# Layer 0 cross-attention: query scaling moved to ScalarE, the second normalisation rewritten as two VectorE operations per tile, beta added to x in advance

## The chip, the core and the metric

The kernel runs on one core of a Trainium2 chip. The metric is the device time of one execution in microseconds (us), given as the median of several executions. Engines are named as in the profile: PE is TensorE's matmul side and PEld its weight loads, DVE is VectorE, ACT is ScalarE, POOL is GpSimd, and SP is SyncE, which here issues DMAs only.

## The reference

The program is a decoder of four layers, each with self-attention, cross-attention and a feed-forward part, on x of 16 batches x 128 tokens x 256 channels in float32. Only the cross-attention of layer 0 is changed. Its part of the reference, where `query` is the layer-normalised x and `key` and `value` are both the context of 16 x 128 x 192:

```python
Qp = query @ Wq + bq
K = _l2norm(key @ Wk + bk)
V = value @ Wv + bv
Q = _l2norm(Qp)
# split into 16 heads of 16
scores = einsum('bhqd,bhkd->bhqk', Q, K) * SCALE        # SCALE = 1/4
attn = softmax(scores, axis=-1)
out = einsum('bhqk,bhkd->bhqd', attn, V)
out = out @ Wo + bo
x = out + Qp
mu = mean(x); var = mean((x - mu) ** 2)
return (x - mu) / sqrt(var + LN_EPS) * ln_gamma + ln_beta
```

The decoder adds the returned value to its own x: `x = x + _L0_xattn_ref(_layernorm(x), ...)`. The length of a query is taken over all 256 channels, before the split into heads.

## The kernel before

**Tiling.** The 16 batches are 16 tiles of 128 tokens (tokens on the partitions, 256 channels along the free side). Four tiles make a group; x lives in SBUF as four buffers `x[0]` to `x[3]`, one for each group, of 128 x 1024 float32 elements. In the built program they appear as x_70, x_72, x_74 and x_76.

**Stages.** `staggered` drives both attentions of layer 0. For each group a generator `prologue(g)` makes keys, values and queries, in pieces that are run between the steps of the group before it. For each tile, `scores16` gives the scores `st` on PE, `exponentials16` the exponentials `e` on ACT (L330, two instructions of 128 x 1024), and `combine16` in four pieces the weighted values `o`, their copy `oT` on ACT (L356), the transposition `o16t`, the division by the row sums on DVE (`rsum` L364, `c` L365), the transposition `ctr`, its copy `cT` on DVE (L373), the product `proj`, and `done(ps)`, which takes the product out of PSUM.

**The prologue of the cross-attention.** `stats` takes mean and variance of x for two groups at a time (L526, L527, buffers `l1mv` and `l1rs`); h is the normalised x (L546). After kT (L555, with the squares `ksq` on ACT, L556), the transposes `tr` of h and the sums of squares of the keys, the queries `qp` = hT x Wq + bq come out of PSUM on DVE (L579), and ACT sums their squares (L580). The reciprocal lengths `n` take a maximum (L583), a square root on ACT (L584) and a reciprocal (L585). `unit` is qp divided by its length, four DVE instructions (L588). POOL then adds bo to qp (L589). PE transposes unit (`utr`), and DVE and ACT write it to `qm`, masked for even and odd heads (L605, L606).

**The end of a group.** `done` adds the product to qp (L616). After the fourth tile, `norm_tokens` normalises qp (L203, L204 for statistics, L193 for the root on ACT, L194 for the reciprocal, L207 for four DVE instructions), and POOL multiplies with gamma (L619), adds beta (L620) and adds the result to x (L621), each in one instruction over the whole group.

**What follows.** `l0_ffn_rows(g)` normalises the new x for the feed-forward part: statistics on DVE (L643, L644), `nmean` (L646), h on ACT (L649), transposes `tr` on PE, and copies `hT` on ACT (L657). It is called for groups 0 and 1 within the cross-attention and for 2 and 3 at the start of the feed-forward part, which then runs gate, up and down products for 33 sets of weights.

**What sets the order.** The functions `pinned` and `pinned_transpose` keep PE in the order in which the program is written. For the other engines a scheduler orders the instructions by a model of when they are ready, and each engine then works through its own queue in order. Small buffers come from a pool (`small`) with four buffers for each name and shape; `bnst` and `bnmv` are such names, shared by `stats` (`bnst` alone), `norm_tokens` and `l0_ffn_rows`. PSUM has four one-bank buffers (`b1`), used in turn by kT, tr, qp, v, utr, o, o16t, ctr and proj, and two two-bank buffers (`b2`) for the scores.

Of the kernel before, what the change touches and what calls it, by code (L numbers as in the profile page):

```python
# [12 lines left out]
AF = mybir.ActivationFunctionType  # L13
ALU = mybir.AluOpType
# [3 lines left out]
P = 128  # L18
B = 16
T = B * P  # L20
DM = 256
DC = 192
NG = 4
GB = B // NG
# [6 lines left out]
class Decoder:  # L31
# [479 lines left out]
    def l0_xattn(self):  # L511
        nc = self.nc
        wq, wk_, wv, wo = self.load4(["L0_xattn_Wq", "L0_xattn_Wk", "L0_xattn_Wv", "L0_xattn_Wo"])
        gamma, beta = self.b("ln_gamma"), self.b("ln_beta")
        T4 = lambda t: slice(t * P, (t + 1) * P)

        rows, qps = {}, []

        def stats(gs):
            n = len(gs)  # L520
            bs = self.small([P, GB, 6], "bnst")
            mv = self.small([P, n, GB, 2], "l1mv")
            rs = self.small([P, n, GB], "l1rs")
            for i, g in enumerate(gs):
                for t in range(GB):
                    nc.vector.bn_stats(bs[:, t, :], self.x[g][:, t, :])  # L526
                    nc.vector.bn_aggr(mv[:, i, t, :], bs[:, t, :])  # L527
            self.rsqrt(rs, mv[:, :, :, 1])
            for i, g in enumerate(gs):
                rows[g] = mv[:, i], rs[:, i]  # L530

        def products(out, pairs):
            for i, (l, r) in enumerate(pairs):
                self.pinned(out, l, r, start=i == 0, stop=i == len(pairs) - 1)

        with self.tc.tile_pool(name="l0x", bufs=1) as wk:
            bq, bv, bo = (self.brow(wk, f"L0_xattn_{n}") for n in ("bq", "bv", "bo"))

            def prologue(g):

                if g in (0, 2):
                    stats([g, g + 1])
                mv, rs = rows[g]
                h = self.hp.tile([P, GB, DM], F, tag="h", name="h", bufs=2)
                for t in range(GB):
                    nc.vector.tensor_scalar(  # L546
                        h[:, t, :], self.x[g][:, t, :], mv[:, t, 0:1], rs[:, t : t + 1], ALU.subtract, ALU.mult
                    )

                kT = wk.tile([P, 2, GT], F, tag="kT", name="kT", bufs=2)  # L550
                sq = self.hp.tile([P, 2, GT], F, tag="hT", name="ksq", bufs=5)
                for half in range(2):
                    ps = self.b1("kT")
                    products(ps, self.ctx_l(wk_, half * P, (half + 1) * P, slice(g * GT, (g + 1) * GT)))
                    nc.vector.tensor_scalar(kT[:, half, :], ps, self.c("L0_xattn_bk")[:, half : half + 1], None, ALU.add)  # L555
                    nc.scalar.activation(sq[:, half, :], kT[:, half, :], AF.Square)  # L556
                    yield
                hT = self.hp.tile([P, 2, GT], F, tag="hT", name="hT", bufs=5)
                for k in range(2):
                    ps = self.b1("tr")  # L560
                    for t in range(GB):
                        self.pinned_transpose(ps[:, T4(t)], h[:, t, k * P : (k + 1) * P])
                    self.evac(hT[:, k, :], ps)

                n = self.small([P, 2, GB], "lengths")
                ps = self.b1("ksum")[:, 0:GB]
                for t in range(GB):
                    products(ps[:, t : t + 1], [(sq[:, half, T4(t)], self.ones[:, 0:1]) for half in range(2)])

                nc.vector.tensor_scalar(n[:, 0], ps, 1e-24, 16.0, ALU.max, ALU.mult)  # L570
                yield
                if g % 2 == 0:
                    qps.append(self.slot([P, 2, GB, DM], "qp"))
                qp = qps[-1][:, g % 2]
                junk = wk.tile([P, DM], BF, tag="junk", name="junk", bufs=1)
                for t in range(GB):
                    ps = self.b1("qp")[:, 0:DM]
                    products(ps, [(hT[:, k, T4(t)], wq[:, k, :]) for k in range(2)])
                    nc.vector.tensor_tensor(qp[:, t, :], ps, bq, ALU.add)  # L579
                    nc.scalar.activation(junk, qp[:, t, :], AF.Square, accum_out=n[:, 1, t : t + 1])  # L580
                    if t == 1:
                        yield
                nc.vector.tensor_scalar(n[:, 1], n[:, 1], 1e-24, None, ALU.max)  # L583
                nc.scalar.activation(n, n, AF.Sqrt)  # L584
                nc.vector.reciprocal(n, n)  # L585
                u = self.hp.tile([P, GB, DM], F, tag="h", name="unit", bufs=2)
                for t in range(GB):
                    nc.vector.tensor_scalar(u[:, t, :], qp[:, t, :], n[:, 1, t : t + 1], None, ALU.mult)  # L588
                nc.gpsimd.tensor_tensor(qp, qp, bo.unsqueeze(1).to_broadcast([P, GB, DM]), ALU.add)  # L589
                yield  # L590
                v = []

                def values(t):
                    pairs = self.ctx_r(wv, 0, DM, slice(g * GT + t * P, g * GT + (t + 1) * P))
                    v.append(self.values32(wk, pairs, bv, products))

                values(0)
                values(1)
                yield
                qm = wk.tile([P, 2, 2, GT], F, tag="qm", name="qm", bufs=2)  # L600
                for half in range(2):
                    ps = self.b1("utr")
                    for t in range(GB):
                        self.pinned_transpose(ps[:, T4(t)], u[:, t, half * P : (half + 1) * P])
                    nc.vector.tensor_scalar(qm[:, half, 0, :], ps, self.par[:, 0:1], None, ALU.mult)  # L605
                    nc.scalar.activation(qm[:, half, 1, :], ps, AF.Copy, scale=self.par[:, 1:2])  # L606
                yield
                values(2)
                values(3)
                return qm, kT, n[:, 0], v, qp  # L610

            def combine(s, g, t, es):
                qp = s[4]

                def done(ps):
                    nc.vector.tensor_tensor(qp[:, t, :], qp[:, t, :], ps, ALU.add)  # L616
                    if t == GB - 1:
                        self.norm_tokens(qp, qp)
                        nc.gpsimd.tensor_tensor(qp, qp, gamma.unsqueeze(1).to_broadcast([P, GB, DM]), ALU.mult)  # L619
                        nc.gpsimd.tensor_tensor(qp, qp, beta.unsqueeze(1).to_broadcast([P, GB, DM]), ALU.add)  # L620
                        nc.gpsimd.tensor_tensor(self.x[g], self.x[g], qp, ALU.add)  # L621

                return self.combine16(wk, es, s[3][t], wo, done)


            self.staggered(
                prologue,
                None,
                lambda s, t: self.scores16(s[0], s[1], T4(t), False),
                lambda s, t, st, nm: self.exponentials16(wk, st, s[2][:, t : t + 1], None),  # L630
                combine,
                {13: [lambda: self.l0_ffn_rows(0)], 14: [lambda: self.l0_ffn_rows(1)]},
            )
# [1944 lines left out]
```

## Time and profile before

| | |
|---|---|
| median of 3 runs | 3607.33 us (3598.66 to 3616.08) |
| profiled execution | 3604.5 us, its span 3602.7 us |
| granted PE clock over the span | 0.962 |
| PE, DVE, ACT, POOL busy | 92%, 59%, 39%, 12% of the span |
| cross-attention of layer 0 | about 181 to 368 us from the span's start |

A position such as "261.55" is in us from the start of the span. In the timeline a line holds start, duration, engine, source line, operation, output and inputs, and in brackets how long the engine sat idle before it and what released it. In the list of groups a line ends with busy us, mean ns of one, and the idle time before the group with what ended most of it. In the windows view each stretch lists the busy us of PE, PEld, DVE, ACT and POOL with the number of instructions, and then the granted PE clock, the DMA share and GB/s. In the list of waits, the numbers are total us, times, and the longest.

### The profile page before, as it was taken

How to read it: one execution, taken by the hardware profiler on the slowest of the kernel's cores; microseconds unless marked ns; L12 is line 12 of the kernel's file. 1: busy time of each engine (PE TensorE's matmuls, PEld its weight loads, DVE VectorE, ACT ScalarE, POOL GpSimd, SP SyncE). 2: the span in 40 equal slices, each digit the busy share in tenths (PEclk: the TensorE clock that was granted, in tenths of full speed). 3: DMA queues.
4: the chain of work that ended last, by engine and by line, in shares of the span. 5: the costliest groups of instructions: out<-in, count | busy, mean ns of one | idle time of the engine just before them, and what ended most of it. 6: DMA issues, size and time to landing. Idle time of an engine off the chain costs nothing.

```text
span 3602.7 us, 51438 instructions
## 1 busy us (share of the span) xinstructions
PE 3305.2 (92%) x20947; PEld 1789.6 (50%) x20947; DVE 2117.7 (59%) x4185; ACT 1415.6 (39%) x1904; POOL 443.5 (12%) x613
## 2 busy tenths in 40 slices
PE   7888999999998899998899999297999999999999
PEld 4655555555556556674455565162222222224656
DVE  5555444444463544558777644426999999963430
ACT  2345311111124422228555323023677767783221
POOL 5422000000003321110000110104000000002100
PEclk9988999999999999999999999597999999999989
DMA  2000000000110100000100000374212020000000
GB/s 77 1 23 10 18 18 18 22 18 18 32 49 2 38 1 1 1 31 20 46 1 13 2 1 1 137 229 126 38 26 32 11 32 12 11 1 26 1 8 18
DMA packets 90500, 105.46 MB, mean 29 GB/s; under 512 B 11380, under 2 KB 72694, under 8 KB 90006
## 3 DMA queue, kind: packets, MB, share of 16 engines
q1 hardware_dynamic: 79672, 89.71, 9.6%
q0 software_dynamic: 4224, 6.43, 0.6%
q10 hardware_dynamic: 6368, 6.03, 0.5%
q8 instruction: 165, 2.70, 0.3%
q14 instruction: 71, 0.58, 0.1%
HBM read 85.53 MB, written 16.60 MB: 28 GB/s over the span
## 4 chain that ended last, share of the span: by engine, by line
PE 78%; DVE 9%; ACT 5%; issue 4%; DMA 2%; POOL 1%; SPq 0%; POOLq 0%; ACTq 0%; DVEq 0%
PE acc L2110 7%; PE down L257 6%; PE gate L257 6%; PE up L257 6%; PE proj L257 6%; PE st L2110 5%; PE one L2110 4%; PE st L257 4%; PE qT L168 4%; PE o L257 3%; PE h L257 2%; DVE mx L2256 2%; PE rb L257 2%; PE fc L168 2%; PE pr L168 2%
## 5 line engine op out<-in xcount | busy, mean ns | idle before, releaser
L2256 DVE TENSOR_REDUCE mx<-one 128x1 f32<-128x512 f32 x1024 | 658.4, 686 | 56.6 <-PE one L2110 47.6
L2393 ACT ACTIVATE e<-st 128x1024 f32<-128x1024 f32 x512 | 497.1, 1021 | 206.5 <-PE st L2110 205.3
L748 ACT ACTIVATE gs<-gate,cols 128x512 f32<-128x512 f32 x132 | 90.7, 687 | 553.1 <-PE gate L257 553.1
L2110 PE MATMUL acc<-e,v 128*32 128x512 f32 x2048 | 283.7, 608 | 1.2 <-ACT e L2393 1.2
L762 DVE SCALAR_TENSOR_TENSOR x<-down,w_all,x 128x256 f32<-128x256 f32 x512 | 212.4, 477 | 110.5 <-PE down L257 110.4
L2110 PE MATMUL st<-qp,kp 113*128 113x512 bf16 x1024 | 270.5, 384 | 5.9 <-DMA qp<-shifts 3.4
L257 PE MATMUL down<-expert,gs 128*128 128x256 f32 x1056 | 250.1, 380 | 2.2 <-DVE gs L749 2.2
L257 PE MATMUL gate<-hT,expert 128*128 128x512 f32 x528 | 250.1, 596 | 0.0
L257 PE MATMUL up<-hT,expert 128*128 128x512 f32 x528 | 248.1, 592 | 0.0
L257 PEld LDWEIGHTS down<-expert,gs 128*128 128x128 f32 x1056 | 200.8, 190 | 85.8 <-issue 61.5
L749 DVE SCALAR_TENSOR_TENSOR gs<-up,cols,gs 128x512 f32<-128x512 f32 x132 | 99.0, 750 | 234.2 <-PE up L257 229.1
L2110 PE MATMUL one<-kp,qp 16*128 16x512 bf16 x1024 | 210.7, 395 | 3.7 <-DVE mx L2256 2.4
L2110 PEld LDWEIGHTS <-qp 16*128 16x128 bf16 x1024 | 48.8, 91 | 326.0 <-issue 321.1
L257 PEld LDWEIGHTS up<-hT,expert 128*128 128x128 f32 x528 | 100.3, 190 | 126.4 <-issue 126.4
L2110 PEld LDWEIGHTS <-kp 113*128 113x128 bf16 x1024 | 78.8, 98 | 142.3 <-issue 80.5
L1120 ACT COPY rb<-rb 128x512 f32<-128x512 f32 x64 | 37.5, 585 | 256.6 <-PE rb L257 256.6
L257 PEld LDWEIGHTS gate<-hT,expert 128*128 128x128 f32 x528 | 100.6, 192 | 70.9 <-issue 64.4
L1122 DVE TENSOR_TENSOR cT<-o,rb 128x512 f32<-128x512 f32 x64 | 44.2, 691 | 154.9 <-ACT rb L1120 154.9
L168 PE MATMUL qT<-hT,L_xattn_Wq 128*128 128x512 f32 x256 | 115.7, 605 | 6.8 <-DVE hT L112 4.5
L257 PE MATMUL o<-e,v 128*32 128x128 f32 (+1 forms) x2048 | 105.4, 279 | 13.7 <-DVE nm L294 11.8
L1429 DVE SCALAR_TENSOR_TENSOR xs<-xBC,cols,xs 128x508 f32<-128x508 f32 x144 | 106.0, 741 | 12.4 <-ACT xs L1425 9.0
L257 PEld LDWEIGHTS o<-e,v 128*32 128x32 f32 (+1 forms) x2048 | 81.5, 124 | 29.7 <-POOL e L335 12.3
(536 smaller groups left out, 5417.3 us busy)
## 6 DMA issues: line engine op xcount, KB each, us to landing
W<-in_L_ffn_W_dram SPq DMA_DIRECT2D x46, 512.0 KB, 5.6
expert<-in_L_ffn_Wg_dram SPq DMA_DIRECT2D x32, 128.0 KB, 2.2
expert<-in_L_ffn_Wu_dram SPq DMA_DIRECT2D x32, 128.0 KB, 2.4
expert<-in_L_ffn_Wd_dram SPq DMA_DIRECT2D x32, 128.0 KB, 2.5
parts<-parts SPq DMA_DIRECT2D x16, 256.0 KB, 3.9
qp<-parts SPq DMA_DIRECT2D x28, 128.0 KB, 3.8
kp<-parts SPq DMA_DIRECT2D x12, 256.0 KB, 8.7
hs<-zero SPq DMA_DIRECT2D x23, 128.0 KB, 1.8
```

The source lines that it names most:

```text
L168: self.nc.tensor.matmul(out, lhsT, rhs, start=i == 0, stop=i == n - 1 and bias is None)
L257: self.tc.keep_in_program_order(self.nc.tensor.matmul(*a, **k))
L748: nc.scalar.activation(gs, pg, AF.Silu, bias=bg)
L749: nc.vector.scalar_tensor_tensor(gs, pu, bu, gs, ALU.add, ALU.mult)
L762: nc.vector.scalar_tensor_tensor(xt, pd[:, t, :], w_all[:, o : o + 1], xt, ALU.mult, ALU.add)
L1120: nc.scalar.copy(rb, ps)
L1122: nc.vector.tensor_tensor(cT, po, rb, ALU.mult)
L1429: stt = lambda *a: pin(nc.vector.scalar_tensor_tensor(*a))
L2110: self.tc.keep_in_program_order(nc.tensor.matmul(*a, **k))
L2256: nc.vector.tensor_reduce(mx[:, t, kc, i : i + 1], pair[i], AX.X, ALU.max)
L2393: nc.scalar.activation(e[:, 2 * p : 2 * p + 2, :], ps, AF.Exp, scale=1.0 / 16.0)
```

## The change

The four instructions that write `unit` move from DVE to ACT. The three POOL instructions at a group's end go. In their place every tile, right after its product is added, takes its statistics and is rewritten as (qp - mean) x gamma on DVE; after the fourth tile the reciprocal deviation is computed, and four DVE instructions add qp x rstd to x. Beta is added to x on POOL in the prologue, after h has been taken from x. The buffers `bnst` and `bnmv` of a group are now taken at its first tile rather than after its fourth.

```diff
-        rows, qps = {}, []
+        rows, qps, norms = {}, [], {}
...
                 for t in range(GB):
-                    nc.vector.tensor_scalar(u[:, t, :], qp[:, t, :], n[:, 1, t : t + 1], None, ALU.mult)
+                    nc.scalar.activation(u[:, t, :], qp[:, t, :], AF.Copy, scale=n[:, 1, t : t + 1])
                 nc.gpsimd.tensor_tensor(qp, qp, bo.unsqueeze(1).to_broadcast([P, GB, DM]), ALU.add)
+                nc.gpsimd.tensor_tensor(self.x[g], self.x[g], beta.unsqueeze(1).to_broadcast([P, GB, DM]), ALU.add)
...
                 def done(ps):
                     nc.vector.tensor_tensor(qp[:, t, :], qp[:, t, :], ps, ALU.add)
+                    if t == 0:
+                        norms[g] = self.small([P, GB, 6], "bnst"), self.small([P, GB, 2], "bnmv")
+                    st, mv = norms[g]
+                    nc.vector.bn_stats(st[:, t, :], qp[:, t, :])
+                    nc.vector.bn_aggr(mv[:, t, :], st[:, t, :])
+                    nc.vector.scalar_tensor_tensor(
+                        qp[:, t, :], qp[:, t, :], mv[:, t, 0:1], gamma, ALU.subtract, ALU.mult
+                    )
                     if t == GB - 1:
-                        self.norm_tokens(qp, qp)
-                        nc.gpsimd.tensor_tensor(qp, qp, gamma.unsqueeze(1).to_broadcast([P, GB, DM]), ALU.mult)
-                        nc.gpsimd.tensor_tensor(qp, qp, beta.unsqueeze(1).to_broadcast([P, GB, DM]), ALU.add)
-                        nc.gpsimd.tensor_tensor(self.x[g], self.x[g], qp, ALU.add)
+                        rs = self.small([P, GB], "rstd")
+                        self.rsqrt(rs, mv[:, :, 1])
+                        for i in range(GB):
+                            xt = self.x[g][:, i, :]
+                            nc.vector.scalar_tensor_tensor(xt, qp[:, i, :], rs[:, i : i + 1], xt, ALU.mult, ALU.add)
```

In the changed file the lines shift a little: unit stays L588, bo on POOL stays L589, beta on POOL is L590, the masked copies are L606 and L607, the addition of the product is L617, the statistics L621 and L622, the multiplication with gamma L623, the addition to x L631. In `l0_ffn_rows` the statistics become L653 and L654, nmean L656 and h L659.

## The prediction

> **What bounds the kernel now.** I read the chain first, then PE's waits in the stage that changes, then the timeline around the longest of them, and last the windows for the granted clock. The chain of the whole execution is PE's:
>
> ```profile
> PE 78%; DVE 9%; ACT 5%; issue 4%; DMA 2%; POOL 1%; SPq 0%; POOLq 0%; ACTq 0%; DVEq 0%
> ```
>
> So only what makes PE wait counts. PE's list of waits from 197 to 370 us has eight rows, 31.2 us together; three carry it:
>
> ```profile
> PE tr L260 <- ACT h L649: 12.8, 2, 7.2
> PE proj L257 <- DVE cT L373: 7.0, 4, 5.4
> PE proj L257 <- DVE rstd L194: 5.4, 1, 5.4
> ```
>
> None of the engines named is short of time; the timeline of the second row shows what is behind it:
>
> ```profile
> 259.96 2.36 POOL L619 TENSOR_TENSOR qp<-qp,bcast 128x1024 f32<-128x1024 f32 x1 [0.66 <-DVE lengths L583]
> 261.55 6.02 DVE L588 TENSOR_SCALAR unit<-qp,lengths 128x256 f32<-128x256 f32 x4
> ...
> 262.40 2.35 POOL L620 TENSOR_TENSOR qp<-qp,bcast 128x1024 f32<-128x1024 f32 x1
> ...
> 264.82 2.34 POOL L621 TENSOR_TENSOR x<-x,qp 128x1024 f32<-128x1024 f32 x1
> ...
> 267.49 0.41 DVE L373 COPY cT<-ctr 128x256 f32<-128x256 f32 x1
> ...
> 268.05 2.05 PE L257 MATMUL proj<-L_xattn_Wq,cT 128*128 128x256 f32 x4 [5.43 <-DVE cT L373]
> ```
>
> Four `unit` instructions take 1.13 us at 196.77 and 6.02 us here, where POOL runs three in a row. They end 2.5 us apart, one per gap between POOL's. cT waits behind them, and PE idles 5.43 us. Group 3 repeats it at 301.76 (6.01 us, PE idle 5.42). `h` (L546) meets L589 at 197.8 and 224.6 (3.42 us instead of 1.38), and nmean (L646) meets L589 at 308.22 (2.06 us) and L619 at 333.29 (2.32 us). At the end of the stage DVE waits for POOL outright, with PE's transposes behind it:
>
> ```profile
> 361.65 2.34 POOL L621 TENSOR_TENSOR x<-x,qp 128x1024 f32<-128x1024 f32 x1
> ...
> 364.02 0.43 DVE L643 BATCH_NORM_STATS2 bnst<-x 128x6 f32<-128x256 f32 x1 [3.10 <-POOL x L621]
> ...
> 365.86 2.81 PE L260 MATMUL tr<-ident,h 128*128 128x128 f32 x8 [7.17 <-ACT h L649]
> ```
>
> An idle PE costs twice, as the windows show. The granted PE clock is the third number from the end of a line (0.58, then 1.00):
>
> ```profile
> 228.00:240.00 12.00, 11.63 (x68) 6.71 (x68) 5.02 (x15) 3.87 (x5) 0.44 (x2) 0.58 0.01 1
> 240.00:262.00 22.00, 22.00 (x213) 15.06 (x216) 10.43 (x32) 12.62 (x22) 3.40 (x7) 1.00 0.00 1
> ```
>
> After 1.8 us idle at 226.5, the next twelve us run at 0.58: eight `v` take 4.27 instead of 2.5 us, sixteen `st` 2.09 instead of 1.15, four `proj` 2.07 instead of 1.13.
>
> **What the Trainium skill says.** "SBUF — State Buffer", section "SBUF: two separate sides": VectorE and GpSimd share a port pair under an exclusive lock; a VectorE operation in a two-port mode, or with two SBUF inputs, and a GpSimd operation exclude each other for a whole instruction, while ScalarE has its own port. The trace agrees: 2.5 us per `unit` beside POOL, and nmean, a 128x4 instruction with two SBUF inputs, takes 2.06. "TensorE: Matmul & The Clock Gate", Part 1: PE's clock halves after a [...]idle window of about 3.4 us. It agrees in kind (0.58 above). "ScalarE: Activation LUTs", section "What ACT_TABLE_LOAD costs": 1283 ns for a load plus about 1380 ns of drain. The trace has 1283 ns, but no drain (at 202.65 the load, at 203.95 the exponential); I use 1.28.
>
> **The change part by part.** Durations are from the profiled execution. I laid the built order of each queue beside the trace and followed it by hand. PE's order is the same in both.
>
> *POOL.* Gone: 12 instructions (L619 to L621) x 2.34 = 28.1 us. Added: 4 beta additions x 2.34 = 9.4. The one for x[0] falls into self-attention, where POOL is idle from 128.6 to 133.42 and h is done at 131.08: it ends at 133.5, cost 0.1 at most. The others follow their h and stand next to L589.
>
> *ACT.* Added: 16 `unit`. Nearest row: h L649, same shape, four in 2.08 us at 335.70. The page named prices a single one at about 0.4 once overlapped, so a group costs 1.6 to 2.1; I take 2.1, together 8.4. They stand between the root of the lengths and the load of the exponential's table, so each group's exponentials come 1.9 to 2.5 us later.
>
> *DVE.* Gone: 16 `unit`, 0.28 each unblocked, 4.5 us, and 16 L207. The 16 L631 cost what L207 did (four in 1.4 us): net zero. New: 16 multiplications with gamma, both tensors in SBUF. No such shape is in the trace; bounds are 0.34 (L207's pitch) and 0.48 (L762, with a PSUM input). I take 0.45, 7.2 us, in a stage where DVE is busy 95 of 172 us. Being of two SBUF inputs, each can still wait for one POOL instruction, 0 to 2.35 us. Queued behind it are the next cT, PSUM copies and qm.
>
> *Moved through the buffers.* As `bnst` is now taken at a group's first tile, the statistics of x[2] and x[3] (8 pairs, 0.54 each) leave the end of self-attention and come after tile 0 of group 0; their root needs two table loads there. Those of x[0] and x[1] for the feed-forward part come after tile 0 of group 2, with two loads between `qm` and the exponentials.
>
> Step by step, where PE gets earlier (+) or later (-):
>
> 1. *End of self-attention:* without L526 between L364 and L365, `c` is 0.28 earlier in three ping-pong rounds: +0.8.
> 2. *Group 0.* The table of the root must now be loaded at 195.15; root 196.43, reciprocal 197.05, unit on ACT 197.1 to 199.2. PE waits from 196.4 to 199.3 instead of 0.8, but h no longer holds qm, whose wait (0.98) goes. The half-clock stretch only moves. `st` at about 202.7 instead of 202.02, and with the rest -0.5.
> 3. *Group 1.* unit 223.35 to 225.45; table; exponentials until 228.85 instead of 226.33. No h stands in DVE's way: L617 at 225.3 instead of 227.91, and `o` starts at 226.6 instead of 228.37. gamma's L623 waits for L589 until 227.9 and holds the second qm. ACT's qm end at 229.55 and 230.8, these release PSUM for the second `v` and for ctr; `st` at 231.35 instead of 234.20, at full clock instead of half. proj ends at 233.6 instead of 238.3: +4.7. The moved statistics (4.3 us on DVE) delay L617 1.6 us and an exponential 3.3 us, both needed only by PE work behind kT: hidden. If kT were shorter, they would show.
> 4. *Group 2* (times as before, shifted by the gain so far). L631 until 260.3; unit 261.15 to 263.25; cT at 261.65, not behind unit; proj 262.65 instead of 268.05; exponentials 264.5 to 266.6. L623 waits for beta's L590 until 268.1, the second qm until 269.35, ACT's until 270.1. `st` at 270.5 instead of 277.24: +6.7, of which 5.4 is the wait.
> 5. *Group 3.* The same without h and beta: `st` at 309.75 instead of 317.64: +7.9.
> 6. *Steps 13 to 16.* The root of x[0]'s statistics and its two loads push the exponentials to 315.6 and nmean and L617 to 314.6; the next `st` comes 6.3 us after the last instead of 4.0 (-2.3), the one after 5.45 instead of 4.9 (-0.5). nmean of x[1] no longer meets POOL: 9.5 instead of 12.5 us to the following `st` (+3.0). L623 and L653 in the last rounds: -0.6. Sum -0.4.
> 7. *Start of the feed-forward part.* x[3] is done at 356.8 instead of 364.0, but router, three loads and statistics now come last: nmean at 361.6 instead of 364.95, hT 2.4 us earlier, then h of x[3] and a load hold the gated product 0.6: +1.8. What is late next is ACT with its tables. After this the weights and PE go on as before.
>
> Sum: 0.8 - 0.5 + 4.7 + 6.7 + 7.9 - 0.4 + 1.8 = **21.0 us**. The profiled execution would come to 3604.5 - 21.0 = 3583.5. Its time is 2.8 below the median of the runs, so for the median I forecast 3607.3 - 21.0, about **3586 us**.
>
> **Rivals.** *The clock keeps the gain small.* The new idle stretches (196 to 199, 269 to 270, 313.7 to 315.6, 326 to 329) set the half clock again. One such stretch cost 1.9 at 202 and 4.8 at 229; two or three more take 9: 12 us gained, 3595. For it: 1.8 us idle were enough at 226.5. Against: 1.4 at 315 were not.
>
> *The change doesn't remove the lock, it moves it.* The 8 POOL instructions left each hold an L623 or L631 for up to 2.35, 18.8 us in all; if most of it reaches PE through cT, 3600 to 3605. Against: L589 and L590 are at most two in a row and stand before tile 1's product, where 16 L623 are spread over 140 us.
>
> *Slower: ACT sets the pace of the groups.* The place is the row of unit, table load and exponentials. If scores wait for their PSUM banks behind it, each group pays its 2.1 us (8.4), the two extra pairs of loads 5.1, each with a half-clock stretch at 4.8 (two: 9.6), against nothing gained if L623 also waits for POOL: +23, about 3630. It decides once an exponential ends later than PE reaches the `st` two tiles on, over some 5 us late; I find 2.5 and 3.3. ACT's share, 89.5 of 172 us, speaks against.
>
> **How the numbers follow.** Half a per cent, 18 us, is about what a measurement of this kernel can tell from no change. The main case (0.70) has its own range 3576 to 3592: unknown prices (gamma 1.6, unit 2) are small, the clock is worth 5 either way; most of it counts as faster by over 0.5% (below 3589.3). The small gain has 0.15, the moved lock 0.08, slower 0.07. For 8 in 10 the range runs from 3571, one more half-clock stretch avoided and the lowest run as base, to 3604, which takes in both smaller gains. Chances: faster 0.70, within 0.5% 0.23, slower 0.07.
>
> **What would show it.** Right: no `unit` on DVE, no DVE instruction of 2.5 us before cT in groups 2 and 3; PE's waits before proj (10.8 us) gone; PEclk near 1.00 where 0.58 stands; POOL 18.7 us less busy. Step 6 is right if `st` follow 6 us apart after group 3. Wrong: L623 at a mean above 1 us, PE waiting for ACT's qm or for `e` more than 2 us in a group, or a difference outside 195 to 375 us.

## The result, and the profile after

| | before | changed |
|---|---|---|
| median of 6 runs each | 3608.64 us (3598.66 to 3616.87) | 3586.05 us (3580.93 to 3597.72) |
| profiled execution, its span | 3604.5, 3602.7 us | 3590.4, 3588.6 us |
| POOL busy | 443.5 us | 424.4 us |

The ratio is 0.994, with a 95% interval of 0.9915 to 0.9964. On another chip the same pair came out at 0.9949 (0.9932 to 0.9966), with medians of 3600.04 and 3581.94. So the medians differ by 23 and 18 us, and the two intervals together run from 12 to 31 us; 21 were forecast. Within that width it is luck that the measured median meets the forecast of about 3586 us to a tenth.

The chain of the changed kernel's execution is PE's as before:

```profile
PE 79%; DVE 10%; ACT 5%; issue 3%; DMA 2%; POOL 1%; SPq 0%; POOLq 0%; ACTq 0%; DVEq 0%
```

PE's waits from 197 to 370 us (us in total, times, longest) are 13.4 us in six rows instead of 31.2 in eight. Two short ones aside (1.0 us), these are left:

```profile
PE tr L260 <- ACT h L659: 7.5, 6, 3.8
PE ctr L260 <- DVE bnmv L622: 2.0, 2, 1.0
PE proj L257 <- DVE cT L373: 1.7, 3, 0.6
PE utr L260 <- ACT unit L588: 1.2, 1, 1.2
```

The two waits of 5.4 us before `proj` are gone, the wait for h is 7.5 instead of 12.8, and a new one stands at the first `utr`. The place in group 2 that the prediction showed now reads so in the timeline (start, duration, instruction, idle time before it):

```profile
264.64 1.70 ACT L588 ACTIVATE unit<-qp,lengths 128x256 f32<-128x256 f32 x4 [0.27 <-DVE lengths L585]
...
265.52 0.42 DVE L373 COPY cT<-ctr 128x256 f32<-128x256 f32 x1
265.87 3.42 DVE L546 TENSOR_SCALAR h<-x,l1mv,l1rs 128x256 f32<-128x256 f32 x4
...
266.43 2.39 POOL L589 TENSOR_TENSOR qp<-qp,L_xattn_bo 128x1024 f32<-128x1024 f32 x1 [3.23 <-ACT unit L588]
...
266.49 1.13 PE L257 MATMUL proj<-L_xattn_Wq,cT 128*128 128x256 f32 x4
...
269.67 1.08 PE L257 MATMUL o<-e,v 128*32 128x128 f32 x32 [0.74 <-DVE qp L617]
```

cT comes 0.1 us after the `st` at 265.42, and `proj` 1.07 us after that `st`; before, it was 6.58 (261.47 to 268.05). h still takes 3.42 us, as L589 runs beside it. The prediction had it free; that costs PE 0.74.

At the start of the feed-forward part PE waited 7.17 us for h before its transposes. Now its timeline reads:

```profile
347.68 2.07 ACT L659 ACTIVATE h<-x,nmean,rstd 128x256 f32<-128x256 f32 x4 [0.41 <-DVE nmean L656]
...
348.33 0.33 PE L260 MATMUL tr<-ident,h 128*128 128x128 f32 x1 [3.00 <-ACT h L659]
```

This part of the gain is not the lock's. Before, DVE stood still until POOL had delivered x (3.10 us), with nmean behind that in its queue; now no POOL instruction stands in this chain.

One thing went against the forecast. The windows of this execution (third number from the end: granted PE clock) show at the start of the stage:

```profile
197.00:226.50 29.50, 29.29 (x128) 16.89 (x132) 6.02 (x12) 10.77 (x16) 5.08 (x4) 0.54 0.00 1
226.50:350.00 123.50, 111.26 (x1080) 75.66 (x1076) 78.05 (x257) 87.86 (x135) 16.84 (x26) 0.98 0.04 11
```

PE is busy for 29.29 of 29.50 us, nearly all of it at half clock: the trace's record of the clock has one stretch of 27.3 us, from 198.5 us on. From there to the second gate product only 5.6 us more are at half clock.

**The stage by interval.** PE's order is the same in all kernels here, so the same PE instruction can be found in every trace. "Group 0" runs from the first `utr` to the `st` at 223.03 of the kernel before, "group 1" from there to its `st` at 261.47, "group 2" to that at 277.24, "group 3" to that at 317.64, "steps 13-16" to the first gate product (353.39), and "start of FFN" to the second (368.45). Half clock is counted from the first `utr` to the second gate product.

| us | group 0 | group 1 | group 2 | group 3 | steps 13-16 | start of FFN | sum | of it at half clock |
|---|---|---|---|---|---|---|---|---|
| before | 25.86 | 38.44 | 15.77 | 40.40 | 35.75 | 15.06 | 171.3 | 43.0 |
| before again | 25.97 | 33.66 | 14.92 | 40.41 | 35.24 | 15.06 | 165.3 | 29.9 |
| changed | 36.35 | 32.14 | 8.14 | 31.78 | 34.69 | 10.90 | 154.0 | 32.9 |
| changed again | 26.63 | 32.15 | 8.14 | 31.79 | 34.72 | 10.90 | 144.3 | 12.4 |
| changed, third | 31.46 | 32.15 | 8.14 | 31.78 | 35.57 | 10.90 | 150.0 | 28.5 |
| unit on DVE | 24.35 | 31.78 | 9.11 | 32.37 | 35.56 | 10.90 | 144.1 | 11.5 |
| unit alone moved | 23.49 | 32.16 | 15.66 | 35.29 | 37.28 | 15.07 | 159.0 | 36.0 |
| own buffers | 23.50 | 32.15 | 11.17 | 32.74 | 33.99 | 10.89 | 144.4 | 15.0 |
| both of these edits | 25.97 | 33.67 | 13.01 | 37.24 | 33.51 | 10.89 | 154.3 | 22.3 |
| one POOL instruction | 25.89 | 38.43 | 9.67 | 37.40 | 37.64 | 12.92 | 162.0 | 37.1 |
| without beta | 23.49 | 32.15 | 8.14 | 31.78 | 34.74 | 10.90 | 141.2 | 8.8 |
| before, split | 28.66 | 33.44 | 12.11 | 36.49 | 34.79 | 16.22 | 161.7 | 33.9 |
| changed, split | 36.34 | 32.14 | 7.45 | 31.79 | 34.83 | 10.90 | 153.5 | 36.1 |
| both edits, split | 24.11 | 38.95 | 12.82 | 37.49 | 33.86 | 10.90 | 158.1 | 32.1 |

In one kernel, an interval that meets the same clock in the same places repeats to 0.1 us. Group 0 of the changed kernel, which met half clock of three lengths, moves by 9.7. What lies outside the stage takes 3430 to 3444 us in these 14 executions, so the stage of one execution does not give the kernel's time.

### The profile page after: what moved, and what is told of

It reads as the page before. It is cut to its first block, busy times and chain, and to the rows that moved or that the text cites. A ratio compares the mean times of both kernels' runs of the same rounds, so it can differ in the third digit from the quotient of the medians.

```text
span 3588.6 us, 51453 instructions
## 1 busy us (share of the span) xinstructions
PE 3314.7 (92%) x20947; PEld 1791.9 (50%) x20947; DVE 2108.9 (59%) x4185; ACT 1428.4 (40%) x1925; POOL 424.4 (12%) x605
## 4 chain that ended last, share of the span: by engine, by line
PE 79%; DVE 10%; ACT 5%; issue 3%; DMA 2%; POOL 1%; SPq 0%; POOLq 0%; ACTq 0%; DVEq 0%
PE acc L2120 7%; PE down L257 6%; PE gate L257 6%; PE up L257 6%; PE proj L257 6%; PE st L2120 5%; PE one L2120 4%; PE qT L168 4%; PE st L257 4%; PE o L257 2%; PE h L257 2%; DVE mx L2266 2%; PE rb L257 2%; PE v L1030 2%; PE fc L168 2%
## 5 line engine op out<-in xcount | busy, mean ns | idle before, releaser
L257 PEld LDWEIGHTS o<-e,v 128*32 128x32 f32 (+1 forms) x2048 | 81.5, 124 | 28.5 <-POOL e L335 12.3
```

What stands on the lines that cost most here:

```text
L257: self.tc.keep_in_program_order(self.nc.tensor.matmul(*a, **k))
```

## The experiments

Theory A: the gain is the end of POOL's long instructions beside DVE. Its rivals: moving unit is what counts; the lock is only moved to other instructions; the clock takes the gain.

### The changed kernel and the kernel before, repeated

> The changed kernel once more, beside the others on one chip. If the gain is that of the sum, 21 us within the spread of the runs, its ratio to the kernel before is 0.992 to 0.997. Theory A says that the 27.3 us at half clock after group 0 follow from PE's idle stretch at 196 to 199 us, where it waits for unit on ScalarE: then this profile shows a half-clock stretch that begins within 4 us of the first st again, though its length may differ. The rival says that this stretch was an accident of that one execution: then it is not there, and st before group 2's unit comes at 256 to 258 us instead of 265.4.

> The kernel before once more, to see what of its profile is the kernel's and what one execution's. Theory A: the row of waits in the stage (tr for h 12.8, proj for cT 7.0 and for rstd 5.4 us) and the times of the first gate product (353.4) and the second (368.5) repeat within 1 us, apart from half-clock stretches that begin in another place by up to 3.4 us and move these times by up to 4 us. Rival: the 10.2 us of half clock at 230 us were the accident of that execution, and without them the second gate product comes 5 us earlier or more.

> The changed kernel a third time, for its profile. Its first execution ran 27.3 us at half clock from 199.1 us on, the second 6.8 us from 199.6 on. Theory A (PE's idle stretch at the first utr opens the half clock[...]): a half-clock stretch begins within 4 us of the first st[...], and the row of waits repeats within 0.5 us. Rival (the long stretch has nothing to do with it): no half clock between 197 and 250 us.

Measured: the changed kernel again 3581.94 us, a third time 3581.2; the row of PE's waits repeats (the one for h with 7.5 and 6.8 us). The half clock of group 0 begins at 199.3 and 199.4 us (at 198.5 in the first profile; the 199.1 and 199.6 in the expectations are too late) and lasts 6.8 and 17.1 us, so it is there in all three executions, with a different length each time. The `st` before group 2's unit came at 255.87 and 260.96 us. The kernel before came out at 3595.79 us with the same long waits (12.9, 7.0 and 5.4 us), but its stage lacked the 10.2 us at half clock on which the prediction's step 3 rested. Before, that stretch showed as 0.58; here the same window is

```profile
228.00:240.00 12.00, 11.65 (x107) 6.22 (x108) 5.88 (x17) 4.98 (x7) 0.88 (x4) 1.00 0.01 1
```

What follows: for this execution the rival of the repeated kernel before was right. Its second gate product came 6.1 us earlier (362.31), about 5 of them in group 1. But the stretch was not the accident of one execution. The version with one POOL instruction, further below, differs from the kernel before only from 259.65 us on, and it has the stretch again in the same place:

```profile
228.00:240.00 12.00, 11.94 (x68) 6.71 (x68) 4.85 (x15) 3.87 (x5) 0.44 (x2) 0.57 0.01 1
```

So after the same PE wait of 1.82 us the half clock came in two of three executions. The stage takes 168.3 us on the mean of two executions before and 149.4 on the mean of three after. That difference of 19 us agrees with the medians.

### Unit back on VectorE; unit alone moved

Two cross edits. The first takes the changed kernel and puts unit back:

```diff
-                    nc.scalar.activation(u[:, t, :], qp[:, t, :], AF.Copy, scale=n[:, 1, t : t + 1])
+                    nc.vector.tensor_scalar(u[:, t, :], qp[:, t, :], n[:, 1, t : t + 1], None, ALU.mult)
```

The second makes the reverse edit to the kernel before and nothing else.

> The changed kernel with unit back on VectorE, everything else kept. Theory A: what held unit on VectorE was three GpSimd instructions in a row, and two of them are gone from that place; unit's four then take 1.1 us in every group instead of 6.0, cT in groups 2 and 3 is not held, and the exponentials come 1 to 2 us earlier than with unit on ScalarE, whose wait of 1.2 us at the first utr is gone. The time is 2 to 10 us below the changed kernel, ratio to the kernel before 0.990 to 0.994. Rival: the move of unit to ScalarE is what brings the gain. Then the proj waits of 5.4 us are back in groups 2 and 3 and the ratio is 0.997 to 1.000.

> The kernel before with only unit moved to ScalarE; the normalisation with its three GpSimd instructions stays. Theory A: the two proj waits of 5.4 us go, since cT is not behind unit, but h, nmean and the wait at the end of the stage (L643 behind L621, PE's transposes 7.2 us) stay, and group 0 pays for unit on ScalarE: gain 0 to 9 us, ratio 0.9975 to 1.000. Rival (the move of unit is the whole effect): ratio 0.993 to 0.996, like the changed kernel. Second rival (the lock only moves to the next VectorE instruction): proj waits for cT over 2 us remain in groups 2 and 3, and the ratio is 1.000 or above.

Measured: unit back on DVE 3579.98 us, ratio to the kernel before 0.9943 (0.9922 to 0.9965), which cannot be told from the changed kernel beside it (0.9949). Unit alone moved: 3600.30 us, 0.9998 (0.9985 to 1.0011), no gain that can be told. With unit on DVE the timeline of group 2 is

```profile
253.99 1.13 DVE L588 TENSOR_SCALAR unit<-qp,lengths 128x256 f32<-128x256 f32 x4
...
255.04 0.42 DVE L373 COPY cT<-ctr 128x256 f32<-128x256 f32 x1
...
255.27 2.36 POOL L589 TENSOR_TENSOR qp<-qp,L_xattn_bo 128x1024 f32<-128x1024 f32 x1 [3.58 <-DVE unit L588]
```

Nothing on POOL runs while unit does, and it takes 1.13 us instead of 6.02. Where only unit has gone to ACT, the same place reads

```profile
253.53 7.75 DVE L546 TENSOR_SCALAR h<-x,l1mv,l1rs 128x256 f32<-128x256 f32 x4
...
254.01 2.36 POOL L620 TENSOR_TENSOR qp<-qp,bcast 128x1024 f32<-128x1024 f32 x1
...
256.45 2.34 POOL L621 TENSOR_TENSOR x<-x,qp 128x1024 f32<-128x1024 f32 x1
258.75 2.39 POOL L589 TENSOR_TENSOR qp<-qp,L_xattn_bo 128x1024 f32<-128x1024 f32 x1
261.21 0.41 DVE L616 TENSOR_TENSOR qp<-qp,proj 128x256 f32<-128x256 f32 x1
...
261.67 1.94 PE L257 MATMUL o<-e,v 128*32 128x128 f32 x32 [5.07 <-DVE qp L616]
```

The three POOL instructions in a row, L620, L621 and L589, now hold h: 7.75 us for four. L616 waits behind h and PE behind L616, 5.07 us, in place of the 5.43 before `proj`. Group 2 takes 15.66 us, as before: there the wait has changed its name and kept its length. In group 3, where no h follows, it did go (35.29 us instead of 40.41), while steps 13 to 16 take 1.5 to 2.0 us more.

What follows: of the change's two halves, the removal of the POOL instructions brings the gain, and moving unit adds nothing measurable to it, alone or with it. For unit alone, 0.9998 lies at the edge of theory A's range and cannot be told from the second rival's 1.000. The waits before `proj` did go, as theory A had it, and in group 2 the lock passed to the next DVE instruction, as the second rival had it. (Its stage took 159.0 us in the one profile, 6.3 less than before again, in groups 0, 1 and 3; its 14 runs show nothing of that, and why is open.) Unit on DVE was forecast 2 to 10 us faster than the changed kernel; the medians are 2.0 apart, with overlapping intervals.

### One POOL instruction instead of three

```diff
-                        nc.gpsimd.tensor_tensor(qp, qp, gamma.unsqueeze(1).to_broadcast([P, GB, DM]), ALU.mult)
-                        nc.gpsimd.tensor_tensor(qp, qp, beta.unsqueeze(1).to_broadcast([P, GB, DM]), ALU.add)
```

> The kernel before without the two GpSimd instructions L619 and L620: the multiplication with gamma and the addition of beta are left out, the addition into x stays on GpSimd, unit stays on VectorE, the statistics are not moved. Theory A (every GpSimd instruction in a row holds VectorE once): in groups 2 and 3 unit meets one instead of three, cT comes 3.5 to 4 us earlier in each, and at the end of the stage x[3] is ready 4.7 us earlier, of which 4 reach PE: first gate product 8 to 10 us earlier (343 to 345), the second 12 to 15 us earlier (354 to 356), ratio 0.995 to 0.998. Rival (a single GpSimd instruction of 2.35 us in that place holds the row as three do, so only their complete removal brings the gain): proj waits for cT of 4 us and more stay, and the second gate product is at most 6 us earlier. Second rival (two instructions fewer are already all of it): 22 us and more.

Measured: 3598.54 us against 3603.60, ratio 0.9977 (0.9965 to 0.9988), within what theory A gave. Its gate products came at 345.87 and 358.79, 0.9 and 2.8 us later than the ends given. In group 2 the timeline has (in this version's file the addition to x is L619)

```profile
259.65 2.35 POOL L619 TENSOR_TENSOR x<-x,qp 128x1024 f32<-128x1024 f32 x1 [0.66 <-DVE lengths L583]
...
261.24 1.70 DVE L588 TENSOR_SCALAR unit<-qp,lengths 128x256 f32<-128x256 f32 x4
```

Unit meets the end of one instruction and takes 1.70 us, where three made it 6.02. Group 2 is 6.1 us shorter than in the first profile of before, group 3 by 3.0, the start of the feed-forward part by 2.1; steps 13 to 16 are 1.9 us longer, with 13.5 us at half clock instead of 6.8. What follows: the number of POOL instructions in the row counts. One is not free either: these three intervals are still 1.5, 5.6 and 2.0 us longer than in the changed kernel. No run does the old normalisation on DVE in its old order, so what the new order of DVE's work adds to the gain is not shown apart.

### Without the addition of beta

```diff
-                nc.gpsimd.tensor_tensor(self.x[g], self.x[g], beta.unsqueeze(1).to_broadcast([P, GB, DM]), ALU.add)
```

> The changed kernel without the addition of beta, which is left out. Theory A: of the four added GpSimd instructions only that of group 2 reaches PE, where h (3.4 us instead of 1.4) and one multiplication with gamma (0.97) wait for it: PE's wait of 0.7 us for L617 in group 2 goes, and the first gate product comes 0.5 to 2.5 us earlier than in the changed kernel's undisturbed execution (330.5). Rival (the lock is moved, not removed, and holds the L623 and L631 throughout): 5 us or more earlier.

Measured: 3582.74 us (one run). The first gate product came at 328.08, 2.4 us earlier than in the changed kernel again, as theory A's number has it, but not for its reason. Groups 1 to 3 take what they took with beta, to 0.01 us. PE's wait of 0.7 us for L617 (L616 in this version's file) stays: h is held by L589, which is still there. The L623 (here L622) that took 0.97 takes 0.47, and nothing on PE waits for it. The whole difference lies in group 0, 23.49 instead of 26.63, where this execution has no half clock:

```profile
197.00:217.00 20.00, 19.01 (x147) 12.17 (x148) 7.94 (x19) 13.62 (x21) 2.79 (x3) 1.00 0.01 2
```

What follows: beta in advance costs nothing in groups 1 to 3, and the moved lock is worth less than 1 us there. Whether its absence or chance kept group 0 at full clock is not settled: PE's wait at the first `utr` was 1.2 us here too.

### Buffers of their own for the second normalisation

```diff
-                        norms[g] = self.small([P, GB, 6], "bnst"), self.small([P, GB, 2], "bnmv")
+                        norms[g] = self.small([P, GB, 6], "nst", bufs=2), self.small([P, GB, 2], "nmv", bufs=2)
```

> The changed kernel with buffers of their own for the statistics of the second normalisation, so that the statistics of x[2] and x[3] go back to the end of self-attention and those of x[0] and x[1] no longer wait for tile 0 of group 2. Theory A: two pairs of table loads (5.1 us of ScalarE) leave groups 0 and 2, the exponentials there come earlier, and the half-clock stretch after group 0 is as in the changed kernel, as unit is still on ScalarE: 1 to 5 us below the changed kernel, ratio to it 0.9985 to 1.000. Rival: the moved statistics were hidden, and the time is the same within 1 us; or worse by 1 us, since c at the end of self-attention comes 0.28 us later in each round.

> Both edits of the two runs above together: the changed kernel with buffers of its own for the statistics of the second normalisation, and unit on VectorE. Theory A (each GpSimd instruction beside VectorE costs, the place of unit costs nothing, the moved statistics cost 1 to 3 us in groups 0 and 2): the first gate product of the feed-forward part starts 23 to 25 us earlier than in the kernel before (353.4), no half-clock stretch between 202 and 250 us, and the time is that of the two versions with one of the edits, 3575 to 3581 where the kernel before takes 3600. Rival: the half clock eats what is saved, since PE then waits elsewhere: the first gate product at 331 or later and 3581 or above.

Measured: own buffers alone 3577.76 us, 0.9936 (0.9912 to 0.9959), 4.2 us below the changed kernel beside it, as forecast, but with overlapping intervals. The forecast that the half clock of group 0 stays was wrong: this execution has none there, and PE's wait at the first `utr` is 0.4 us instead of 1.2 (its list of waits from 190 us on):

```profile
PE utr L260 <- ACT unit L588: 0.4, 1, 0.4
```

With unit on DVE as well 3588.49 us, 0.9952 (0.9934 to 0.9971), on a chip where the kernel before takes 3603.60. The forecast for both edits was wrong in the time and in the stage: its first gate product came at 339.90, not at 328 to 330, half clock lies at 202.2 to 205.6, where none was forecast, and PE waits for L617 in three groups, so that the rival's numbers were met:

```profile
PE o L257 <- DVE qp L617: 5.7, 3, 2.6
```

With the statistics back in their old place, those of x[0] (L653) stand on DVE ahead of the L617 of group 2, behind an h that L589 has held:

```profile
257.60 3.38 DVE L546 TENSOR_SCALAR h<-x,l1mv,l1rs 128x256 f32<-128x256 f32 x4
...
260.90 0.74 DVE L653 BATCH_NORM_STATS2 bnst<-x 128x6 f32<-128x256 f32 x2
...
262.35 0.40 DVE L617 TENSOR_TENSOR qp<-qp,proj 128x256 f32<-128x256 f32 x1
```

What follows: the shared buffers, which move these statistics behind the first tile of a group, help group 2 (8.14 us against 11.17, of which 1.7 may be the clock: by an estimate, half of the 3.4 us at half clock there). Group 0 takes 26.6 to 36.3 us in the changed kernel and 23.5 here, but the difference is time at half clock: the version without beta shares the buffers too, has no half clock there and takes 23.49. Whether the shorter wait at the first `utr` kept the clock up, one execution does not settle. The two edits do not add up. None of the three versions is shown to beat the changed kernel.

### POOL's instructions split in four

```diff
-                nc.gpsimd.tensor_tensor(qp, qp, bo.unsqueeze(1).to_broadcast([P, GB, DM]), ALU.add)
+                for i in range(GB):
+                    nc.gpsimd.tensor_tensor(qp[:, i, :], qp[:, i, :], bo, ALU.add)
```

and so for every POOL instruction of 128x1024 in the stage: in the kernel before, in the changed kernel, and in the version with both edits.

> The kernel before with each of its GpSimd instructions of 128x1024 in this stage (L589, L619 to L621) issued as four of 128x256; nothing else changed. Theory A (VectorE waits for one whole GpSimd instruction at a time): the same GpSimd work now holds VectorE about 0.6 us at a time, so four unit in groups 2 and 3 take 2.4 to 3.6 us instead of 6.0, PE's waits of 5.4 us before proj fall below 3 us, h in groups 0 to 2 takes under 3 us; at the end of the stage GpSimd starts on the first tile while L207 works on the second, x[3] is ready up to 1 us earlier. Gain at the second gate product 4 to 12 us, ratio 0.9965 to 0.999. Rival (what counts is how long GpSimd works beside VectorE, not in how many instructions): unit takes 6 us as before, gain under 2 us; a loss if the fixed time of an instruction makes four of them longer than 2.35 us together by 1 us or more.

> The changed kernel with its two GpSimd instructions of 128x1024 per group (L589, L590) issued as four of 128x256 each. Theory A: h in group 2 falls from 3.4 to about 2 us and the L623 that waits there no longer takes 0.97, but only 0.7 us of PE's waiting in the stage hangs on it: 0 to 2 us at the second gate product, ratio to the kernel before as the changed kernel's, 0.994 to 0.997. Rival (the lock was moved to h, L623 and L631 and holds the groups back): 5 us or more over the changed kernel, ratio 0.990 to 0.9935.

> The version with unit on VectorE and buffers of its own for the second normalisation's statistics, with L589 and L590 issued as four each. In the unsplit version PE waited 5.7 us in three groups for L617, which stood behind h (3.4 us beside L589) and the statistics of x[0]. Theory A: h no longer meets a whole 2.35 us instruction, these waits fall to 1.5 to 3 us and the second gate product comes 3 to 8 us earlier than in the unsplit version (350.8), at 343 to 348; ratio to the kernel before 0.992 to 0.995. Rival: L617 waits for the statistics that stand ahead of it whatever GpSimd does, and the waits stay above 4.5 us.

Measured: before, split 3607.27 us against 3604.72, ratio 1.0006 (0.9994 to 1.0019); changed, split 3586.40, 0.9953 (0.9938 to 0.9968); both edits, split 3595.03, 0.9969 (0.9953 to 0.9985). In the split kernel before, group 2 reads (gamma, beta and the addition to x are L621, L623 and L625 there)

```profile
260.50 3.00 DVE L588 TENSOR_SCALAR unit<-qp,lengths 128x256 f32<-128x256 f32 x4
...
261.12 2.23 POOL L623 TENSOR_TENSOR qp<-qp,bcast 128x256 f32<-128x256 f32 x3
...
263.42 0.41 DVE L373 COPY cT<-ctr 128x256 f32<-128x256 f32 x1
...
263.98 2.02 PE L257 MATMUL proj<-L_xattn_Wq,cT 128*128 128x256 f32 x4 [3.06 <-DVE cT L373]
```

Unit takes 3.00 us, one instruction per gap, and each gap is now 0.75 us. The waits before `proj` fall from 5.4 to 3.1 and 3.0, where less than 3 was forecast. This is the clearest sight of the lock that the Trainium skill describes ("SBUF — State Buffer", "SBUF: two separate sides"): it is held for one instruction, so each DVE instruction that meets it waits for what is left of one POOL instruction, as long as POOL has more of them. But a quarter takes 0.74 us and not 0.585, so POOL works 26% longer, and L207 meets POOL now too (653 ns on the mean instead of 414). The start of the feed-forward part takes 1.2 us more: POOL's last addition ends 0.3 us later after the first gate product, and DVE's queue then has the router's instructions between the statistics of x and nmean. The stage of this one execution was still 3.6 us shorter than before again; the time is not, so the forecast gain was missed, and where the rest went is open. In the changed kernel the split takes 0.7 us off group 2 (7.45) and changes nothing else, as theory A had it; its rival falls. In the version with both edits group 2 hardly changes (12.82 against 13.01), as L617 (L619 in this version's file) still waits behind the statistics; and since POOL can start after the first quarter of unit, it now runs beside unit itself, whose mean is 586 ns, against 349 in the version with only unit on DVE. The forecasts of 343 to 348 for its second gate product (357.36) and of 0.992 to 0.995 for its ratio were missed. The run doesn't keep to either theory: the waits for L617 came to 4.3 us, between the two.

## Why the prediction was right, point by point

The mechanism was right where it matters most: with the POOL instructions the two waits of 5.4 us went, and the one at the start of the feed-forward part fell from 7.2 to 3.0. That the sum was right is in part luck. It forecast 21.0 us; the stage gives 11.3 to 27.0, according to which executions before and after are paired, and 19 on the means. By the same means, steps 2 to 7 come to -5.6, +3.9, +7.2, +8.6, +0.5 and +4.2, so errors of up to 5 us cancelled.

- **Step 1, +0.8.** PE reaches the first `utr` at 196.93 to 197.35 in the three executions, against 197.17 and 197.05. It arrives earlier and then waits 1.2 us for unit: at most 0.2 is left.
- **Step 2, -0.5, was the mis-sized term.** "The half-clock stretch only moves" is wrong. It lasted 3.4 us in both profiles of before and 27.3, 6.8 and 17.1 us after, and group 0 cost 10.4, 0.7 and 5.5 us, 5.5 on the mean. The wait ahead of it, forecast from 196.4 to 199.3 us, measures 1.2 us, from 195.8 on.
- **Step 3, +4.7.** Against the first profile of before it is 6.3, against the second 1.5. The working took full clock instead of half as a sure gain; the half clock was there in two of three executions. What the kernel gained is that L617 no longer waits behind h: `o` follows `utr` after 0.97 us, before again it took 2.85.
- **Step 4, +6.7.** 6.8 against the second profile, 7.6 against the first. The wait of 5.4 us went as forecast. h was blocked after all, for 0.74 us of PE's time, and L623 cost less.
- **Step 5, +7.9.** 8.6.
- **Step 6, -0.4.** +1.1 in the first pair of profiles, by its parts: -0.9 for the `st` that comes 4.9 us after the last (305.34, 310.25), where 6.3 was forecast; -0.5 for the one after it, as forecast; +1.9 instead of +3.0 at nmean of x[1] (10.65 us to the following `st`, not 9.5); +0.6 instead of -0.6 for the last rounds.
- **Step 7, +1.8, came out at +4.2.** h and the transposes are as much earlier as nmean is, and PE waited for no gated product, for which the working took off 0.6: the second gate product comes 2.60 us after the transposes' start, as it did before (2.59).
- **Prices.** Unit on ACT 1.70 us for four (2.1 taken, 1.6 the lower end). L623 0.52 on the mean, one of 0.97 (0.45 taken). L631 1.67 for four, against 1.38 for L207, called equal. POOL 19.1 us less busy (18.7 forecast).
- **The rivals.** "The clock keeps the gain small" came true in the first execution's group 0 and less in the others. "The lock is moved, not removed" is false of the change (0.7 us) and true of unit's move alone. ACT never set the pace: no PE wait over 0.3 us for ACT's qm, none listed for `e`.

The prediction credited the removal of the 5.4 us waits without saying which of the two halves of the change did it. The cross edits say so: either half empties the place before `proj`, but in group 2 only the removal of POOL's instructions leaves little to wait for behind it.

## What to carry to other kernels

When a stalled DVE instruction is moved to another engine, ask what stands next in DVE's queue while GpSimd still runs: in group 2 the wait of 5.4 us came back as one of 5.1 on other instructions, and only fewer GpSimd instructions removed it. Before a half-clock stretch of a profile is booked as a gain, look for it in further profiles of the same kernel; here it was worth 5 us and was there in two of three. Buffers that two uses share also move instructions in the queues (here to the good of group 2), so edits that are harmless one by one have to be run together.

## What the runs showed of the hardware

- In the changed kernel a wait of 1.2 us on PE was followed by 6.8 to 27.3 us at half clock, though PE was busy, as the profile counts it, for 29.29 of 29.50 us in the first of these. The Trainium skill ("TensorE: Matmul & The Clock Gate", Part 1) gives about 3.4 us of sustained work as enough for full clock. The stretches of 6.8 and more in the changed kernel do not agree with this; why they lasted so long stays open.
- The waits ahead of a half-clock stretch were shorter than the window of 3.4 us that the prediction took from that page: 0.8 us at the first `utr` and 1.0 at the `st` before 3.4 us at half clock, and 1.8 before 10.2.
- The wait at the first `utr` does not decide it alone: with unit on VectorE PE waited 1.0 us, and with beta left out 1.2, and no half clock followed in either. Where it was only 0.4 (own buffers, unit alone moved) none followed; where it was 1.2, half clock followed in four of five executions.
- The addition on POOL takes 2.35 us for 128x1024 and 0.74 for 128x256, so a quarter of the size takes 31% of the time.
- Within the 25 runs of the kernel before on one chip, the time and the mean granted clock move together, by 2.8 us for each 0.001 of clock. So most of the spread of 25 us among them goes with time at half clock, and differences of 5 us between two kernels need many runs.
